# A four-layer graph kernel: the 20-key block in the middle of a part, sums copied head by head, small products as rows, more kept blocks, and two softmax layers in one loop

## The chip, the core and the metric

The kernel runs on one core of one Trainium2 chip. Its time is the device time of one execution in microseconds (us); a kernel's time is the median of several executions. Engines are PE (TensorE), DVE (VectorE), ACT (ScalarE), POOL (GpSimd) and SP (SyncE); the last two are used here mostly to issue DMAs.

## The reference, cut to what matters

`x` is 2708 x 512, `adj` a 0/1 matrix of 2708 x 2708 with ones on its diagonal. Four layers follow each other, each of the form `x = layernorm(x + layer(x, adj))`:

```python
# layer 0, H = 4 heads of width 128; both attention patterns are adj
Xw  = einsum('hnd,hde->hne', Xh, W)
f1  = einsum('hnd,hd->hn', Xw, V[:, 0, :, 0]); f2 = einsum('hnd,hd->hn', Xw, V[:, 1, :, 0])
sig = sigmoid(f1[:, :, None] + f2[:, None, :])
att = masked_softmax(adj * sig)                      # both halves of ALPHA are equal
Xn  = batchnorm(att @ Xw)                            # first pass over att
emb = batchnorm(elu(Xn @ Wenc.T + b) + Xn)
Y   = elu((att @ emb) @ W.T)                         # second pass over att
out = batchnorm(elu(Y @ Wdec.T + b) + Y)
# layer 1
A @ (x @ W + b) / deg[:, None]
# layer 2: h = x @ edge_w, scores h @ h.T, masked by adj, softmax, times node_att and adj
adj * node_att * softmax(where(adj > 0, h @ h.T, NEG_BIG)) @ (x @ weight) + bias
# layer 3
softmax(query @ key.T * scale + adj + adj) @ (x @ Wv + bv)
```

## The kernel before

All matrices are cut into NT = 22 blocks of 128 rows; the last has 20 rows. Layer 0 works in transposed form: a block of 128 keys against half of the queries (HW = 1354 columns, in three chunks of 452, 452 and 450, one PSUM bank each), for two heads at a time. A half and a pair of heads make a *part*; a pass has four of them, in the order (half 0, heads 0-1), (half 0, heads 2-3), (half 1, heads 0-1), (half 1, heads 2-3). In the text `p` is 0 or 1 for the pair of heads.

`project` (L199) computes the values `xw` for the 22 blocks, the rows f1 and f2, and the tile `f1b` in which f1 is spread over all partitions; for the first part this is made by six matmuls (L223). Rows of f1 are also written to `f1_d` in DRAM, from where the later parts load them spread out.

`attention_pass` (L285) runs twice. For each key block it *forms* a tile `t` of 128 x 2 x 1354 (`form`, L309): two Tanh on ACT (L341, the sigmoid written as tanh), one scalar_tensor_tensor on DVE with the block `a` of the adjacency (L349), one Exp on ACT (L350). There are four `t` buffers. In the first pass and for p = 0 the adjacency block comes from the input and is changed first on DVE (L330, L331), then written to `adj_d` on POOL's queue; otherwise it comes from `adj_d`. The blocks listed in `KEPT` are written to DRAM in pass 1 (POOL's queue) and loaded in pass 2 on SP's queue instead of being formed (L390).

Then the products of the block: for each of two heads and three chunks one matmul into `po` (L397), each recorded as two PE instructions[...]. In pass 1 the row sums of `t` come on top (`psm`, L420): for p = 0 of each block; for p = 1 of the first `ALONE` = 6 blocks alone, and after that of two blocks added on DVE (L414). The `po` banks are used by all parts, so a part can begin only when those of the part before have been read.

The reader of `po` is `keep` in pass 1 (L491: six copies, odd chunks on ACT, even ones on DVE, L499) and `decode` in pass 2 (L684: six `take` on DVE, L702). What they leave for later (`scaled`, or `shifted` L715, `turn` L724 and `mlp` L733 with `elu` L431) is done one piece a block in the next part. At the end of the second part of pass 1 `keep` also makes a small matrix-vector product (`small_product` L467: 16 matmuls 128 x 1); two more are made between the passes (`ps_u`, `ps_mean`), where TensorE also transposes and multiplies layer 3's query and key weights (L586, L614) and runs the first dense layer (L637). The last part of pass 2 has no next part: its takes, turns and dense layer run by themselves. Then layer 1's weights are loaded, multiplied with ones (`ps_w1`), centred by four DVE instructions (L847), and the last batch norm is worked out (`batch_scale`, `batch_shift` L461).

Layer 1 starts with L896 (transposes) and L118 (rows times weights), a loop over the adjacency follows (L954).

`softmax_layer` (L1024) is called for layer 2 and again for layer 3, each time with its own pools. It has 7 groups of query blocks and for each 22 key blocks, 154 steps. Scores of a step (L1106; in layer 2 a part of them transposed from scores kept in DRAM, L1098) run 25 steps ahead of the sums of the same group and key (L1213), as the maximum over all keys has to be known. `key_order` puts the 20-row block in the middle. `finish3` writes layer 3's rows on POOL's queue (L1464), from a tile `y` with two buffers.

The order of each engine's work is set by a scheduler that follows the order of the program; an instruction can be tied to another with `tc.issue_after`.

Of the kernel before, what the change touches and what calls it, by code (L numbers as in the profile page):

```python
# [17 lines left out]
P = 128  # L18
# [11 lines left out]
def gnn_stack_kernel(  # L30
# [35 lines left out]
    Q = 32  # L66
# [10 lines left out]
    nc.sync.dma_start(prm_sb, prm)  # L77
# [49 lines left out]
    assert HW <= HB * BANK and NT * P - N < P  # L127
# [14 lines left out]
    ALONE = 6  # L142


    KEPT = [(5, 13, 21), (3, 9, 15, 21)]
# [10 lines left out]
    with ExitStack() as l0:  # L156
# [31 lines left out]
        nc.vector.tensor_scalar(bm1, prm_sb[:, MB_DEC, :], 1.0, None, ALU.subtract)  # L188
        w0T_sb = p0.tile([P, H, P], F32, name="w0T_sb")
        nc.sync.dma_start(w0T_sb, w0T)  # L190
# [8 lines left out]
        def project(att, psum):  # L199
# [5 lines left out]
            nc.sync.dma_start(w0x[:, :, :P], w0)  # L205
            v12 = att.tile([P, H, 2], F32, tag="v12", name="v12", bufs=1)
            nc.sync.dma_start(v12[:, :, 0], v1)
            nc.sync.dma_start(v12[:, :, 1], v2.rearrange("(h e) -> e h", h=H))
            for c in range(C):
                nc.sync.dma_start(xT_sb[:, c, :], xT[c * P : (c + 1) * P, :])  # L210
# [6 lines left out]
            wv1 = held[:, H * (P + 2) : H * (2 * P + 2)].rearrange("p (h e) -> p h e", h=H)  # L217
            nc.vector.tensor_copy(wv1, w0x[:, :, P : P + 1].to_broadcast([P, H, P]))
            f1b = att.tile([P, HP, HW], F32, tag="f1b", name="f1b")
            for k in range(HP):  # L220
                for q, (q0, w) in enumerate(HCH[0]):
                    pf = psum.tile([P, HP, BANK], F32, tag=f"po{q}", name="pf")[:, k, :]
                    nc.tensor.matmul(  # L223
                        pf[:, :w], wv1[:, k, :], xT_sb[:, k, q0 : q0 + w], start=True, stop=True
                    )
                    copy = nc.scalar.copy if q % 2 else nc.vector.tensor_copy
                    copy(f1b[:, k, q0 : q0 + w], pf[:, :w])
            for ci, (c0, w) in enumerate(CHUNKS):
                pf = psum.tile([P, BANK], F32, tag=f"psm{ci % 2}", name="pf")
                for h in range(H):  # L230
                    nc.tensor.matmul(
                        pf[32 * h : 32 * h + 32, :w],
                        wv1[:, h, :32],
# [4 lines left out]
                f1c = att.tile([P, BW], F32, tag="rs", name="f1c")  # L238
                nc.vector.tensor_copy(f1c[:, :w], pf[:, :w])
                nc.gpsimd.dma_start(f1_d[:, c0 : c0 + w], f1c[0 : 32 * H : 32, :w])  # L240
            for jt, (j0, n) in enumerate(BLOCKS):
                pxw = psum.tile([P, H // HP, BANK], F32, tag=f"po{jt % HB}", name="pxw")
                pv = pxw[:, :, : HP * (P + 2)].rearrange("p a (k e) -> p a k e", k=HP)
                for h in range(H):
# [16 lines left out]
                    None,  # L261
                    ALU.mult,
                )
            copies(xw[:, NT - 1, :])
            copies(f2h[:, NT - 1, :])
            return f1b

# [324 lines left out]
        with (  # L592
# [248 lines left out]
            for ci in early:  # L841
                load_x(ci)
# [695 lines left out]
```

## Time and profile before

| | |
|---|---|
| median of 3 executions | 3347.64 us (3344.58 to 3348.74) |
| profiled execution | 3344.3 us, span 3342.5 us, mean granted clock 0.987 |
| first product of pass 1 (L397) | starts at 52.71 us |
| pass 1, to the last 20-row block | 569 us |
| pass 2, to the last part's own work | 692 to 1148.8 us |
| layer 1's first transpose (L896) | 1219.62 us |
| layer 2's softmax | 1684 to 2366.8 us |
| layer 3's first instruction on PE | 2373.57 us |
| last PE work | 3332 us |

The span is the time from the first to the last instruction that the profile records. In the page, the group lines of section 5 give line, engine, operation, tiles, count, then busy time and mean ns of one, and the idle time before them with what ended it. PEclk in section 2 is the clock that TensorE was granted, in tenths of full speed: below 9, the same matmul takes longer. A matmul of 452 columns takes 0.379 us per record at the full clock, counted from start to start.

### The profile page before, as it was taken

What the parts mean: (1) busy time and instruction counts of PE and PEld (TensorE: products, weight loads), DVE (VectorE), ACT (ScalarE), POOL (GpSimd) and SP (SyncE); (2) the same over time, 40 slices, a digit from 0 to 9 for tenths busy, and PEclk for the clock granted to TensorE, in tenths of its full rate; (3) what the DMA queues carried; (4) which work ended last, traced back from release to release, by engine and by line L of the source; (5) the groups of instructions that cost most, each with busy time, mean ns of one, the idle gap of its engine ahead of it and who ended that gap; (6) DMA issues with size and microseconds to landing.
All of it is one profiled execution on the core that took longest, in us unless ns stands there. A gap on an engine that the chain in (4) does not pass through costs nothing.

```text
span 3342.5 us, 30573 instructions
## 1 busy us (share of the span) xinstructions
PE 3251.5 (97%) x10980; PEld 1741.6 (52%) x10980; DVE 1988.9 (60%) x3227; ACT 1347.6 (40%) x1518; POOL 130.7 (4%) x212
## 2 busy tenths in 40 slices
PE   8999999999999989999999999999999999999998
PEld 5444444544444445885555555444455555555554
DVE  7868978767687585445135677776253443443533
ACT  6888887468877652001133333332011010110110
POOL 1100100000000000000010000000000000000001
PEclk9999999999999999999999999999999999999999
DMA  7655753335535412540044444553211111111100
GB/s 284 248 172 187 275 195 102 121 106 185 187 126 166 152 40 76 144 129 15 0 129 127 122 129 131 148 146 95 70 44 36 42 33 42 40 34 45 33 23 20
DMA packets 168576, 367.58 MB, mean 110 GB/s; under 512 B 20870, under 2 KB 111710, under 8 KB 165032
## 3 DMA queue, kind: packets, MB, share of 16 engines
q1 hardware_dynamic: 153448, 301.77, 30.2%
q0 software_dynamic: 14976, 63.86, 5.1%
q8 instruction: 86, 1.41, 0.2%
q14 instruction: 66, 0.54, 0.0%
HBM read 301.67 MB, written 63.35 MB: 109 GB/s over the span
## 4 chain that ended last, share of the span: by engine, by line
PE 72%; issue 13%; DVE 9%; DMA 3%; ACT 3%; POOL 1%; SPq 0%; POOLq 0%; DVEq 0%; ACTq 0%
PE po L1213 21%; PE ps_s L1106 17%; PE po L397 9%; PE ps_nb L954 6%; PE ps_wide L1015 4%; DVE t L349 3%; PE ps_hid L118 2%; PE ps_sup L1356 2%; PE ps_o L1291 2%; PE ps_mlp L637 1%; DMA a<-adj_d 1%; PE ps_dec L733 1%; ACT t L341 1%; DMA a_cols<-in_adjT_dram 1%; ACT t L350 1%
## 5 line engine op out<-in xcount | busy, mean ns | idle before, releaser
L349 DVE SCALAR_TENSOR_TENSOR t<-t,a 128x2708 f32<-128x2708 f32 (+1 forms) x162 | 480.0, 2975 | 142.4 <-ACT t L341 140.4
L341 ACT ACTIVATE t<-f1b,f2h 128x1354 f32<-128x1354 f32 (+1 forms) x324 | 445.8, 1414 | 87.9 <-PE psm L420 42.7
L350 ACT ACTIVATE t<-t 128x2708 f32<-128x2708 f32 (+1 forms) x162 | 396.7, 2452 | 71.1 <-DVE t L349 69.7
L397 PE MATMUL po<-t,xw 128*128 128x452 f32 (+3 forms) x1056 | 416.2, 557 | 8.1 <-ACT t L350 4.0
L397 PE MATMUL po<-t,emb 128*128 128x452 f32 (+3 forms) x1056 | 404.4, 552 | 16.7 <-ACT t L350 9.0
L1213 PE MATMUL po<-sup,e 128*128 128x512 f32 x882 | 410.3, 602 | 5.5 <-DVE e L1400 5.3
L1213 PE MATMUL po<-e,xs 128*128 128x384 f32 (+1 forms) x1176 | 407.5, 489 | 0.0
L1106 PE MATMUL ps_s<-q,hT 128*128 128x384 f32 (+1 forms) x1176 | 403.5, 489 | 0.0
L1454 DVE SCALAR_TENSOR_TENSOR e<-a_cols,ps_s 128x384 f32<-128x384 f32 (+1 forms) x154 | 85.6, 556 | 419.3 <-PE ps_s L1106 396.2
L397 PEld LDWEIGHTS po<-t,emb 128*128 128x128 f32 (+1 forms) x1056 | 195.6, 192 | 218.9 <-issue 195.0
L1106 PEld LDWEIGHTS ps_s<-q,hT 128*128 128x128 f32 x1176 | 222.6, 190 | 161.5 <-issue 6.5
L397 PEld LDWEIGHTS po<-t,xw 128*128 128x128 f32 (+1 forms) x1056 | 190.8, 192 | 220.6 <-issue 201.8
L1213 PEld LDWEIGHTS po<-e,xs 128*128 128x128 f32 x1176 | 221.6, 190 | 157.2 <-issue 6.0
L1213 PEld LDWEIGHTS po<-sup,e 128*128 128x128 f32 x882 | 161.6, 192 | 176.4 <-issue 149.6
L98 ACT ACTIVATE ln_rstd<-ln_rstd 128x1 f32<-128x1 f32 x88 | 17.2, 201 | 494.1 <-DVE ln_rstd L97 493.5
L1106 PE MATMUL ps_s<-hT 128*128 128x384 f32 (+5 forms) x672 | 212.3, 461 | 2.4 <-DVE e L1397 1.7
L1396 ACT ACTIVATE a_cols<-a_cols,neg_big 128x384 f32<-128x384 f32 (+1 forms) x154 | 94.8, 617 | 239.1 <-DMA a_cols<-in_adjT_dram 202.2
L954 PE MATMUL ps_nb<-hid_hi,at 128*128 128x512 f32 x484 | 185.6, 390 | 1.1 <-DVE at L947 1.1
L954 PE MATMUL ps_nb<-hid_lo,at 128*128 128x512 f32 x462 | 179.9, 389 | 0.0
L1190 ACT COPY nmax<-pb 128x384 f32<-128x384 f32 (+1 forms) x14 | 6.7, 480 | 424.9 <-PE pb L1177 345.6
L1208 DVE TENSOR_TENSOR acc<-acc,e 128x384 f32<-128x384 f32 (+2 forms) x294 | 162.5, 553 | 12.2 <-ACT e L1198 2.3
L1106 PEld LDWEIGHTS ps_s<-hT 128*128 128x128 f32 x672 | 122.4, 190 | 88.3 <-issue 17.8
(237 smaller groups left out, 3494.4 us busy)
## 6 DMA issues: line engine op xcount, KB each, us to landing
a<-adj_d SPq DMA_DIRECT2D x116, 677.0 KB
a_cols<-in_adjT_dram SPq DMA_DIRECT2D x378, 192.0 KB
a<-in_adjT_dram SPq DMA_DIRECT2D x42, 677.0 KB
adj_d<-a POOLq DMA_DIRECT2D x42, 677.0 KB, 4.6
raw<-in_adjT_dram SPq DMA_DIRECT2D x105, 256.0 KB
kept<-t POOLq DMA_DIRECT2D x10, 1354.0 KB, 6.5
t<-kept SPq DMA_DIRECT2D x10, 1354.0 KB
a_cols<-in_adjT_dram SPq DMA_DIRECT2D x63, 202.0 KB
```

The source lines that it names most:

```text
L118: nc.tensor.matmul(ps[:n], xt[:, c, :n], w[:, c, :], start=(c == 0), stop=(c == C - 1))
L341: nc.scalar.activation(tv[:, k, :], f1b[:n, k, :w], AF.Tanh, bias=f2h[:n, jt, h : h + 1], scale=0.5,)
L349: nc.vector.scalar_tensor_tensor(tv, tv, GUARD, ab, ALU.add, ALU.mult)
L350: nc.scalar.activation(tv, tv, AF.Exp, scale=0.5)
L397: nc.tensor.matmul(po[HB * k + q][:, :qw], values[r : r + n, jt, h * P : (h + 1) * P], t[r : r + n, k, q0 : q0 + qw], start=(jt == 0), sto ...
L954: nc.tensor.matmul(pos[it], at, half[:, jt, :], start=(jt == 0 and k == 0), stop=(jt == NT - 1),)
L1015: nc.tensor.matmul(ps[:, :width], w(c, o), xt(c), start=(c == 0), stop=(c == C - 1),)
L1106: nc.tensor.matmul(ps[:, b * P : w], keys[:, c, j0 : j0 + P], st["q"][:, c, b * P :], start=(c == 0), stop=(c == C - 1),)
L1208: nc.vector.tensor_tensor(acc, acc, e[:m], ALU.add)
L1213: nc.tensor.matmul(out, lhsT, rhs, start=(k == 0), stop=(k == NT - 1))
L1396: nc.scalar.activation(a, a, AF.Identity, bias=neg_big[: a.shape[0]], scale=1.0e30)
L1454: nc.vector.scalar_tensor_tensor(e, a, 2.0, ps, ALU.mult, ALU.add)
```

## The change

- `project`: the inputs are loaded in another order, `xT` in six column chunks with two adjacency blocks between them. The six spreading matmuls go; f1's rows of the first half are written to `f1_d` and loaded back spread over the partitions. Values of 17 blocks come first; those of the other five, and f1 of the second half, after the first block's DVE step.
- `ORDER`: the 20-row block is taken in place 11 of each part instead of last. `ALONE` is 4, and the last two blocks are also summed alone (`LAST`).
- The form at place 2 is issued after the PSUM copies of the part before (`taken`); the load of `f1b` for the next part after an earlier adjacency load.
- `KEPT`: five places for each pair of heads, one of them the 20-row block: 16 full blocks kept instead of 10.
- `small_product` makes a row of 512 first, copies it, and turns it by four matmuls.
- In the last part `turn` uses the `po` banks, and `centre` (layer 1's weights) runs within it; four groups of layer 1's first instructions are issued after `batch_shift`.
- `softmax_layer` gives back its two step functions. One loop runs both layers; layer 3's scores start 12 steps after layer 2's last score. Layer 3's tiles lie in buffers that layer 2 has left. Its first group takes the keys in their natural order; `y` has four buffers, and the last group's rows leave on SP's queue.

```diff
+    ORDER = list(range(NT // 2)) + [NT - 1] + list(range(NT // 2, NT - 1))
-    ALONE = 6
+    ALONE, LAST = 4, 2
-    KEPT = [(5, 13, 21), (3, 9, 15, 21)]
+    KEPT = [(4, 8, 11, 14, 18), (3, 7, 11, 15, 19)]
+    KEPT = [[ORDER[k] for k in places] for places in KEPT]
...
-            for k in range(HP):
-                for q, (q0, w) in enumerate(HCH[0]):
-                    pf = psum.tile([P, HP, BANK], F32, tag=f"po{q}", name="pf")[:, k, :]
-                    nc.tensor.matmul(
-                        pf[:, :w], wv1[:, k, :], xT_sb[:, k, q0 : q0 + w], start=True, stop=True
-                    )
-                    copy = nc.scalar.copy if q % 2 else nc.vector.tensor_copy
-                    copy(f1b[:, k, q0 : q0 + w], pf[:, :w])
+            for ci, (q0, _) in enumerate(HCH[0]):
+                f1_rows(ci, stage[:, q0:])
+            nc.sync.dma_start(f1_d[:, h0 : h0 + w], stage[0 : 32 * H : 32, :w])
+            spread = nc.sync.dma_start(
+                f1b[:, :, :w], f1_d[:HP, h0 : h0 + w].partition_broadcast(P)
+            )
...
+            AT_ONCE = NT - 5
+            for jt in range(AT_ONCE):
+                values_of(jt)
+
+            def rest(step):
+
+                with tc.issue_after(step.ins):
+                    for jt in range(AT_ONCE, NT):
+                        values_of(jt)
...
-                    for jt, (j0, n) in enumerate(BLOCKS):
+                    for place, jt in enumerate(ORDER):
...
-                            form(hf, p, jt, att, prepare, f1b, t[:rows, :, :w])
+                            with ExitStack() as order:
+
+                                for ins in taken.values() if place == 2 else ():
+                                    order.enter_context(tc.issue_after(ins.ins))
+                                step = form(hf, p, jt, att, prepare, f1b, t[:rows, :, :w])
...
-                        if prepare or jt < ALONE or (jt % 2 == 0 and jt + 1 == NT):
+                        if prepare or not ALONE <= place < NT - LAST:
...
-        def small_product(ps, w, v):
-
+        def small_product(ps, w, v, row):
+
+            for c in range(C):
+                nc.tensor.matmul(
+                    ps[:1, :F], v[:, c : c + 1], w[:, c, :], start=(c == 0), stop=(c == C - 1)
+                )
+            nc.vector.tensor_copy(row, ps[:1, :F])
             for o in range(C):
-                for c in range(C):
-                    nc.tensor.matmul(
-                        ps[:, o : o + 1],
-                        w[:, c, o * P : (o + 1) * P],
-                        v[:, c : c + 1],
-                        start=(c == 0),
-                        stop=(c == C - 1),
-                    )
-            return ps
+                nc.tensor.matmul(
+                    ps[:, o : o + 1],
+                    row[:, o * P : (o + 1) * P],
+                    ones[:1, 0:1],
+                    start=True,
+                    stop=True,
+                )
+            return ps[:, :C]
...
-                        copy(
+                        taken[q % 2] = copy(
                             ft[:, HP * p + k, h0 + q0 : h0 + q0 + qw], po[HB * k + q][:, :qw]
                         )
...
+                    ps = po[HB * k + q]
+                    if not final:
+                        ps = psum.tile([P, BANK], F32, tag="misc", name="ps_y", bufs=2)
...
                     mlp(q, 2, st, True)
+                    if q == 0:
+                        centre(po[0])
                     mlp(q, 3, st, True)
...
+        with tc.issue_after(ready[0].ins):
+            nc.vector.memset(hid_hi[:, NT - 1, :].bitcast(F32), 0.0)
...
-            y = att.tile([P, F], F32, tag="y", name="y3")
+            y = room(17 + it % 4, 1, F)
...
-                nc.gpsimd.dma_start(out[i0 : i0 + n, :], y[:n])
+                queue = nc.sync if it in GROUPS[-1] else nc.gpsimd
+                queue.dma_start(out[i0 : i0 + n, :], y[:n])
...
+        steps = len(GROUPS) * NT
+        lag = NT + AHEAD
+        start3 = steps + 12
+        for t in range(start3 + steps + lag):
+            if t == steps:
+                weights3()
+            if t == steps + lag:
+                values3()
+            if t < steps:
+                score2(t)
+            elif 0 <= t - start3 < steps:
+                score3(t - start3)
+            for first, step in ((lag, sum2), (start3 + lag, sum3)):
+                if 0 <= t - first < steps:
+                    step(t - first)
```

## The prediction

> **What bounds the kernel now.** I read the page's busy times and slices first, then the windows by stage, the groups by line, the waits and time lines around each dark slice, and the chain last.
>
> ```profile
> PE 3251.5 (97%) x10980; PEld 1741.6 (52%) x10980; DVE 1988.9 (60%) x3227; ACT 1347.6 (40%) x1518; POOL 130.7 (4%) x212
> PE   8999999999999989999999999999999999999998
> ...
> 176.00:192.00 16.00, 15.02 (x71) 6.07 (x64) 9.50 (x10) 13.30 (x10) 1.17 (x2) 0.79 0.44 134
> ...
> 305.00:325.00 20.00, 19.74 (x82) 12.29 (x83) 14.46 (x16) 11.67 (x10) 2.24 (x4) 0.66 0.46 153
> ...
> 692.00:1148.80 456.80, 439.35 (x1170) 216.04 (x1172) 329.63 (x269) 372.87 (x246) 1.06 (x2) 0.98 0.48 156
> 1148.80:1220.00 71.20, 60.04 (x156) 28.72 (x151) 61.94 (x108) 23.53 (x40) 0.00 (x0) 0.96 0.31 107
> ...
> 2366.80:2382.00 15.20, 8.68 (x27) 5.51 (x26) 8.23 (x30) 3.36 (x9) 4.67 (x6) 0.66 0.73 229
> ```
>
> TensorE is the bound: 97%, leaving 91 us idle. The window rows (length, then PE, PEld, DVE, ACT, POOL busy, granted clock, DMA share, GB/s) show that this is not all. At the seams of layer 0's parts (176, 305) PE counts as busy, but at a clock of 0.79 and 0.66. The change removes almost no matmul, so its worth lies in idle gaps and half-rate stretches.
>
> ```profile
> PE po L397 <- ACT t L350: 9.0, 6, 2.6
> PE po L397 <- DVE ot L702: 7.8, 3, 3.3
> ...
> 737.65 2.06 PE L397 MATMUL po<-t,emb 128*128 128x452 f32 x5
> 741.84 4.12 PE L397 MATMUL po<-t,emb 128*128 128x452 f32 x6 [2.13 <-ACT t L350]
> ...
> 1039.63 2.25 PE L397 MATMUL po<-t,emb 128*128 128x450 f32 x13
> 1044.86 7.64 PE L397 MATMUL po<-t,emb 128*128 128x452 f32 x13 [2.98 <-DVE ot L702]
> ```
>
> These are waits and PE time lines of pass 2. Two things stop PE: the formed block is late (ACT), or the sums of the part before have not left PSUM (L702). After a stop the next few records take twice their 0.379 us. Counting starts of matmuls against that pitch, a seam costs in all: pass 1 5.3, 8.9 and 5.9 us; pass 2 5.6, 5.9 and 6.3 us; stalls inside pass 2's parts 4.1, 1.0, 1.0, 1.2 and 4.2 us.
>
> ```profile
> L349 DVE SCALAR_TENSOR_TENSOR t<-t,a 128x2708 f32<-128x2708 f32 (+1 forms) x162 | 480.0, 2975 | 142.4 <-ACT t L341 140.4
> L341 ACT ACTIVATE t<-f1b,f2h 128x1354 f32<-128x1354 f32 (+1 forms) x324 | 445.8, 1414 | 87.9 <-PE psm L420 42.7
> L350 ACT ACTIVATE t<-t 128x2708 f32<-128x2708 f32 (+1 forms) x162 | 396.7, 2452 | 71.1 <-DVE t L349 69.7
> ```
>
> Forming a block takes ACT 2 x 1.414 + 2.452 = 5.28 us; pass 2's products take PE 12 x 0.379 = 4.55 us. In a part with 19 formed blocks (p = 0) ACT needs 100.3 us plus about 4 for six Exp of the elu, PE 21 x 4.55 + 1.8 = 97.4 plus about 4.6. ACT is the slower one there.
>
> ```profile
> 1212.81 2.48 DVE xs L847 x4
> ...
> 1215.42 0.48 DVE hid_hi L867
> ...
> 1215.94 1.11 DVE w_sb L876
> ...
> 1219.62 0.45 PE tp_out L896
> ...
> 2373.57 3.45 PE L1005 MATMUL tp<-ident,xs 128*128 128x128 f32 x16 [6.21 <-DVE xs L113]
> ```
>
> Chain and time line: layer 1's weights are centred on the path into layer 1, and layer 3 starts only when layer 2's last normalization is over.
>
> **The change part by part.** Gains against the profiled execution of 3344.3 us (span 3342.5), which lies 3.3 us under the median.
>
> *Start.* Six spreading matmuls (12 records x 0.379 = 4.5 us) go; the rows come back by a broadcast DMA of 1354 KB. PE's first L397 was at 52.71 us, with two blocks' sums (2.75 us) already done: effectively 49.96. Inputs arrive in column chunks, so values start earlier, and only 17 of 22 blocks' values stand ahead of the first product. The new wait is f1b by DMA. From inputs moving at the row's 269 GB/s I estimate f1b at 29.6, the first L349 at 35.5, the first product at 44: gain 6. Bounds: 9 if the broadcast is early; 2 if it comes 4 us late (two adjacency blocks stand ahead of it on SP's queue, the next ones behind). A kept or adjacency write on POOL is not in the way: f1's first half now goes through SP.
>
> *Pass 1 seams.* Before, the last block has 20 rows, 1.79 us of PE instead of 4.55, so the copies L499 get no cover, and ACT's three of them (0.48 each) stand behind Tanh of the next part. After: 20 rows at place 11, the last two blocks summed alone, and the form at place 2 waits for the copies. Banks come free 3.0, 3.8 and 4.55 us into a full last block; two 0.6 us DVE or 0.48 us ACT copies each end at about 5.8 us, under the 1.4 us of row sums that follow. Left: 1 us a seam, and 3 at the second, where the small product sits. As rows it takes PE the same 3.4 us (4 x 512 columns) but at full clock, plus a DVE copy of 0.6 and its semaphores, 1.5 to 2 on a path that nothing covers. Gains 4 + 6 + 5 = 15; the pass's end (1.85 and 1.63 us gaps, part stays) 2; stalls inside p = 1 parts 3. What the added wait delays: ACT's place-2 form, by about 2 us, with all later forms behind it. In p = 1 parts ACT has 117 us of work against PE's 116, so I take 2 us back for each of two such parts: -4. Six more kept writes on POOL hold a t buffer about as long as the existing ones (Tanh waited for such a write 5.5 us in all, ten writes): under 3 us on ACT, covered by PE. Pass 1: 16 (10 to 25).
>
> *Middle.* The two small products as rows, without the half rate after 128x1 matmuls (4.93 us for eight records at 602.8): 2 (0 to 5).
>
> *Pass 2.* Six forms fewer: ACT -31.7 us, DVE -17.9 us. A p = 0 part goes from 19 to 17 forms, 89.8 + 4 on ACT against PE's 102: the bound is PE. The longest run of formed blocks falls from 7 (7 x 0.73 = 5.1 us lost to PE) to 4 (2.9), with up to three blocks in hand. The 20 rows in the middle take PE 1.8 us but are a kept block in every part. Stalls of 11.5 go to about 3: gain 8.5. Seams: before, L702 queued behind L349; with a full block last and 4.55 us of PE ahead the six takes (0.62 each) start earlier. Nothing covers their first pair: PE went on 1.43 us after the takes began (797.73 to 799.16). So 17.8 becomes 3 x 1.4 = 4.2: gain 13.5. Together 22 (12 to 27).
>
> *Rule against row.* The Trainium skill, "TensorE: Matmul & The Clock Gate", Part 1 "The HAM clock gate", says the array drops to half clock after about one 3.4 us window without work, and then runs some 3.4 us at half rate. By it the stops of 2.13 and 2.98 us above would cost only themselves. The rows disagree: six records took 4.12 us behind 2.13 us idle, thirteen 7.64 behind 2.98. On pass 2's stops the slow records alone add 9.5 us. By the rule pass 2 gains 14, by the rows 22; I take the rows. Stops up to 1.13 us left full rate, so the 1.4 us I leave at each seam should stay cheap.
>
> *Last part.* w1's product (3.43 us) and its four L847 (2.48) move among the elu work of the last part. PE has 11 us idle there and takes the product for nothing; DVE is busy 61.94 of 71.2 us, so of 2.48 I charge 1.5 (up to 5 if PE's product also lies on the path). L847, the memset 0.48, the copy 1.11 and two L947 (0.75) leave the path: 4.8, of which I count 3.1 since the copy is still needed. The takes start 1.5 us earlier and the 2.33 us stop with its half rate (4.1) shrinks by 2.5: 3.1 + 2.5 - 1.5, net 4 (0 to 8). turn() in po banks instead of misc frees two PSUM banks; I count nothing for it, as the takes release po just ahead.
>
> *Layers 2 and 3 in one loop.* Layer 3's scores start before layer 2's sums end, so the 10.8 us lost at 2366.8 go (6.37 gap, the rest half rate): 9 (7 to 10.5). The reordered weight loads come hundreds of us after their buffers are free. L3's first spread of maxima (6.6 lost) stays.
>
> *Tail.* Four y buffers remove a POOL wait of 1.8 us that was mostly hidden, the last stores leave by SP: 1.5 (0.5 to 2.5).
>
> Layer 1 and the other groups: order unchanged, 0.
>
> Sum: 6 + 16 + 2 + 22 + 4 + 9 + 1.5 = 60.5. 3344.3 - 60.5 = 3283.8; plus 3.3 to the median: 3287.
>
> **The rivals.** *Seams stay.* Takes and copies again stand behind an L349, stops stay over 2 us, half rate with them. For it: DVE is 72% busy in pass 2, in order. Against it: the explicit wait at place 2. Pass 1 and 2 then give 10 instead of 38: gain about 32, 3315.
>
> *The change doesn't do what it says.* The waits end at another instruction than those named, so only the start, the merge and the tail count: 16.5, 3331.
>
> *Slower: kept reloads become exposed.* Sixteen reloads of 1354 KB on SP's in-order queue each wait for a t buffer, with the next adjacency loads behind them. A buffer frees three blocks (13.65 us) before its use; these DMAs land in 5.4 us (median; at most 9.8). Exposure starts at 13.65, and the kernel turns slower when the mean exposure passes 60.5 / 16 = 3.8 us, a landing of 17.4 us. At 20 us: 16 x 6.35 = 102 lost, 3389. Against it: pass 2 moves 156 GB/s at a DMA share of 0.48 and would rise to about 165.
>
> **How the numbers follow.** Differences under about 0.2% (6.7 us) can't be told from none. Main case 0.63, 3266 to 3300; seams stay 0.22, 3300 to 3325; only start, merge, tail 0.09, about 3331; a near cancellation 0.03; exposed reloads 0.03. Faster 0.94, same 0.03, slower 0.03. The range takes the main case's edge from below (3262: unknown costs at their good ends) and most of the seams case: 3262 to 3320.
>
> **What would show it.** Right: granted clock near 1.00 where the parts meet; no L702 or L499 wait over 1.5 us; layer 1's first product (1219.62 before) at about 1170, earlier by the 50 us of layer 0's parts; no gap before layer 3's first product; ACT under 350 us busy in pass 2. Wrong: first L397 after 50 us; PE waiting for a t loaded from DRAM; ACT as releaser inside p = 1 parts of pass 1 for more than 4 us; the last part longer than 71 us.

## The result: 27 us faster, less than half of what was forecast

| | before | changed | ratio, 95% interval |
|---|---|---|---|
| median | 3346.11 us (4 executions) | 3318.66 us (4) | 0.9921 [0.9905, 0.9937] |
| profiled execution's span | 3342.5 us | 3317.5 us | |

The changed kernel ran once more among the last experiments: 3320.15 us, 0.9917 [0.99, 0.9933]. The forecast was 3287. The number of the rival "seams stay" (3315) is near, but of its six seams only two went its way, and the largest loss was another.

Lines of the page of the changed kernel, then of its windows, its waits in pass 1 and in the stretch after that, and its PE time line:

```profile
PE 3232.7 (97%) x10920; PEld 1725.2 (52%) x10920; DVE 1971.7 (59%) x3221; ACT 1319.5 (40%) x1497; POOL 130.1 (4%) x211
```

```profile
172.90:190.00 17.10, 17.10 (x80) 7.57 (x80) 11.87 (x7) 16.38 (x11) 1.74 (x3) 1.00 0.58 180
299.00:319.00 20.00, 10.99 (x36) 4.39 (x27) 15.99 (x17) 9.48 (x6) 2.56 (x5) 0.74 0.52 168
692.90:1140.20 447.30, 434.92 (x1173) 213.89 (x1173) 313.37 (x265) 343.78 (x228) 1.05 (x2) 0.99 0.51 172
1140.20:1204.80 64.60, 57.12 (x150) 27.84 (x148) 59.05 (x104) 23.84 (x41) 0.00 (x0) 0.96 0.29 99
2398.00:2414.00 16.00, 16.00 (x66) 9.04 (x66) 12.48 (x40) 4.43 (x10) 2.44 (x3) 1.00 0.15 38
```

```profile
PE po L460 <- ACT t L394: 15.7, 6, 8.2
PE psm L483 <- DVE t L477: 3.7, 3, 1.4
```

```profile
PE po L460 <- ACT t L394: 9.1, 7, 5.8
PE tp_out L985 <- DVE ot L979: 7.5, 1, 7.5
PE po L460 <- DVE ot L814: 3.2, 1, 3.2
```

For comparison, two waits of the kernel before in its start and pass 1 (50 to 600 us):

```profile
PE po L397 <- ACT t L350: 4.0, 7, 1.0
PE po L397 <- ACT ft L499: 4.0, 2, 3.1
```

The windows show both sides. Pass 1's first seam (172.9) has full clock and no idle time, and so has the place where layer 2 meets layer 3 (2398): those two are repaired. The second seam (299) is worse than before, with PE busy 11 of 20 us. In the waits of pass 1, products that wait for a formed block (L460 for L394) have taken the place of products that wait for the sums to leave PSUM. The waits of pass 2 look the same, but their longest one (5.8 us) is put down to the wrong engine, as shown below.

By stages, from starts of matmuls (in the start and pass 1, 2.75 us of row sums that lay ahead of the first product before are counted as pass 1; parts are in the order of the text):

| stage | before | changed | difference | forecast |
|---|---|---|---|---|
| to the first product of pass 1 | 50.0 | 43.3 | -6.7 | -6 |
| pass 1 | 521.9 | 528.6 | +6.7 | -16 |
| middle | 120.1 | 121.0 | +0.9 | -2 |
| pass 2, four parts | 107.2, 109.9, 135.8, 104.0 | 108.0, 107.9, 128.3, 103.1 | -9.5 | -22 |
| last part, to layer 1's first transpose | 70.8 | 64.7 | -6.1 | -4 |
| layer 1 | 304.1 | 304.7 | +0.6 | 0 |
| from layer 1's end to layer 3's first sums | 950.7 | 944.6 | -6.1 | -9 |
| layer 3 to its last projection | 857.2 | 857.2 | 0 | 0 |
| after that | 10.9 | 6.2 | -4.7 | -1.5 |

But for rounding, the differences add up to the 25.0 us between the two spans. Two rows carry the error: pass 1 (22.7 us) and pass 2 (12.5 us).

### The profile page after: what moved, and what is told of

The parts are those of the page before. It is cut to its first block, busy times and chain, and to the rows that moved or that the text cites. A ratio compares the mean times of both kernels' runs of the same rounds, so it can differ in the third digit from the quotient of the medians.

```text
span 3317.5 us, 30401 instructions
## 1 busy us (share of the span) xinstructions
PE 3232.7 (97%) x10920; PEld 1725.2 (52%) x10920; DVE 1971.7 (59%) x3221; ACT 1319.5 (40%) x1497; POOL 130.1 (4%) x211
## 4 chain that ended last, share of the span: by engine, by line
PE 76%; DVE 9%; issue 8%; DMA 4%; ACT 3%; POOL 0%; SPq 0%; DVEq 0%; POOLq 0%; ACTq 0%
PE po L1310 22%; PE ps_s L1203 17%; PE po L460 11%; PE ps_nb L1044 6%; PE ps_wide L1105 4%; DVE t L393 3%; PE ps_hid L117 2%; PE ps_sup L1447 2%; PE ps_o L1388 2%; PE ps_mlp L713 2%; PE ps_dec L848 2%; DMA a<-adj_d 1%; ACT t L394 1%; DMA a_cols<-in_adjT_dram 1%; PE psm L483 1%
## 5 line engine op out<-in xcount | busy, mean ns | idle before, releaser
L393 DVE SCALAR_TENSOR_TENSOR t<-t,a 128x2708 f32<-128x2708 f32 (+1 forms) x156 | 462.1, 2974 | 125.0 <-ACT t L385 121.1
L385 ACT ACTIVATE t<-f1b,f2h 128x1354 f32<-128x1354 f32 (+1 forms) x312 | 428.1, 1413 | 61.7 <-PE po L460 28.0
L460 PE MATMUL po<-t,xw 128*128 128x452 f32 (+3 forms) x1056 | 415.1, 557 | 15.7 <-ACT t L394 15.7
L394 ACT ACTIVATE t<-t 128x2708 f32<-128x2708 f32 (+1 forms) x156 | 382.5, 2454 | 110.5 <-DVE t L393 110.3
L460 PE MATMUL po<-t,emb 128*128 128x452 f32 (+3 forms) x1056 | 400.3, 547 | 12.4 <-ACT t L394 9.1
L1203 PE MATMUL ps_s<-sup,hT 128*128 128x384 f32 (+1 forms) x1176 | 406.9, 490 | 0.0
L460 PEld LDWEIGHTS po<-t,xw 128*128 128x128 f32 (+1 forms) x1056 | 191.2, 192 | 228.4 <-issue 201.7
L1203 PEld LDWEIGHTS ps_s<-sup,hT 128*128 128x128 f32 x1176 | 221.9, 190 | 164.2 <-issue 14.1
L460 PEld LDWEIGHTS po<-t,emb 128*128 128x128 f32 (+1 forms) x1056 | 193.5, 190 | 212.1 <-issue 187.3
L1294 DVE TENSOR_TENSOR e<-e,nmax 128x384 f32<-128x384 f32 (+1 forms) x308 | 154.5, 551 | 21.8 <-ACT nmax L1287 21.8
```

Of the source, the lines that this page charges most:

```text
L385: nc.scalar.activation(tv[:, k, :], f1b[:n, k, :w], AF.Tanh, bias=f2h[:n, jt, h : h + 1], scale=0.5,)
L393: step = nc.vector.scalar_tensor_tensor(tv, tv, GUARD, ab, ALU.add, ALU.mult)
L394: nc.scalar.activation(tv, tv, AF.Exp, scale=0.5)
L460: nc.tensor.matmul(po[HB * k + q][:, :qw], values[r : r + n, jt, h * P : (h + 1) * P], t[r : r + n, k, q0 : q0 + qw], start=(place == 0), ...
L1203: nc.tensor.matmul(ps[:, b * P : w], keys[:, c, j0 : j0 + P], st["q"][:, c, b * P :], start=(c == 0), stop=(c == C - 1),)
L1294: nc.vector.tensor_tensor(e, e, st["nmax"][:, :w], ALU.add)
```

## The experiments

Every edit is against the changed kernel unless it is said otherwise. The table gives the stages that differ, in us, from the profile of each; "(1)" is a single execution. Profiles of kernels with the same pass 1 show how far its second part varies by itself (137.2 to 139.9).

| kernel | pass 1, four parts | middle | pass 2, four parts | median | ratio to before |
|---|---|---|---|---|---|
| changed | 129.6, 139.9, 132.3, 126.8 | 121.0 | 108.0, 107.9, 128.3, 103.1 | 3318.66 | 0.9921 [0.9905, 0.9937] |
| e1 row out of z | 129.6, 127.0, 132.7, 126.2 | 120.6 | 108.1, 107.9, 128.4, 102.9 | 3312.18 | 0.9889 [0.9874, 0.9904] |
| e2 20 rows last in pass 1, p = 1 | 129.6, 131.5, 132.2, 118.8 | 124.0 | 108.2, 108.1, 128.3, 103.2 | 3307.57 | 0.9878 [0.9862, 0.9895] |
| e4 places 10 and 11 alone | 129.6, 136.2, 131.7, 123.9 | 120.3 | 108.2, 109.4, 128.3, 103.0 | 3313.89 | 0.9895 [0.9880, 0.9910] |
| e5 = e1 and e2 | 129.9, 118.6, 139.0, 117.7 | 124.4 | 108.4, 107.9, 128.4, 103.1 | 3302.67 | 0.9864 [0.9848, 0.9881] |
| e8 no added wait | 129.6, 142.9, 133.5, 125.9 | 121.1 | 108.2, 109.5, 129.4, 103.0 | 3321.58 | 0.9919 [0.9904, 0.9934] |
| e3 other kept places | 130.9, 139.8, 132.7, 126.5 | 120.7 | 106.0, 106.6, 128.8, 103.1 | 3323.94 | 0.9929 [0.9915, 0.9944] |
| e6 20 rows last in pass 2 | 129.6, 139.1, 132.2, 124.3 | 121.2 | 105.5, 109.6, 134.3, 105.4 | 3326.14 | 0.9934 [0.9919, 0.9949] |
| e7 10 kept | 129.6, 137.2, 132.7, 126.3 | 120.8 | 110.5, 107.2, 138.1, 108.1 | 3335.22 | 0.9962 [0.9949, 0.9975] |
| e9 last rows by POOL | 129.7, 137.2, 132.8, 126.5 | 120.9 | 108.2, 109.2, 128.0, 103.0 | 3323.33 (1) | |
| e10 middle's products in columns | 129.7, 137.3, 132.7, 126.3 | 121.7 | 108.0, 109.4, 129.7, 102.8 | 3318.20 (1) | |
| e11 no counting | 129.8, 137.3, 132.8, 126.6 | 118.2 | 106.0, 109.2, 128.7, 102.7 | 3315.37 (1) | |
| e12 = e5, takes first | 129.6, 118.6, 138.6, 117.9 | 123.7 | 103.9, 106.9, 131.0, 108.2 | 3302.30 | 0.9870 [0.9852, 0.9887] |
| e13 = e5, last of p = 0 kept | 129.6, 118.6, 139.9, 117.7 | 122.9 | 105.7, 110.5, 128.5, 103.9 | 3300.34 | 0.9858 [0.9843, 0.9873] |
| e14 = e13, six kept for p = 1 | 129.6, 124.2, 134.4, 117.9 | 122.8 | 105.5, 113.1, 129.5, 102.1 | 3299.66 | 0.9858 [0.9840, 0.9876] |
| e16 = e13, no counting | 129.6, 118.5, 138.8, 117.7 | 121.1 | 102.9, 107.2, 128.4, 102.6 | 3291.13 (1) | |
| e17 = e13, counting in pass 1 | 137.3, 121.9, 146.9, 122.7 | 120.6 | 102.9, 107.2, 128.1, 102.6 | 3314.98 | 0.9893 [0.9875, 0.9910] |

### Pass 1: a shared buffer, and a short block in the middle

The second seam of the changed kernel, first DVE, then PE (start, length, instructions, and in brackets the idle time before and what ended it):

```profile
284.44 2.97 DVE L393 SCALAR_TENSOR_TENSOR t<-t,a 128x2708 f32<-128x2708 f32 x1
296.56 1.16 DVE L569 COPY ft<-po 128x452 f32<-128x452 f32 x2 [9.15 <-PE po L460]
...
302.78 0.68 DVE L538 COPY row<-po 1x512 f32<-1x512 f32 x1 [2.70 <-PE po L535]
304.59 0.16 DVE L575 TENSOR_TENSOR enc_bias<-po,prm_sb 128x4 f32<-128x4 f32 x1 [1.14 <-PE po L540]
304.68 0.87 DVE L374 TENSOR_SCALAR z<-a 128x1354 f32<-128x1354 f32 x1
305.58 1.57 DVE L375 SCALAR_TENSOR_TENSOR a<-z,a 128x1354 f32<-128x1354 f32 x1
```

```profile
303.51 1.05 PE L540 MATMUL po<-ones,row 1*128 1x1 f32 x8 [0.77 <-DVE row L538]
312.80 6.31 PE L460 MATMUL po<-t,xw 128*128 128x452 f32 x12 [8.24 <-ACT t L394]
```

DVE stands idle for 9.15 us and prepares the next half's first block (L374, L375) only when the small product is over. Before, that preparation (L330 there) ran while the last blocks of the part were multiplied, ahead of the copies:

```profile
301.47 0.86 DVE L330 TENSOR_SCALAR z<-a 128x1354 f32<-128x1354 f32 x1
...
305.14 1.14 DVE L499 COPY ft<-po 128x452 f32<-128x452 f32 x2
```

The row of the new small product is a tile with the tag of `z`, of which there is one buffer: the next writer of `z` has to wait until the row is read. From 304.68 the chain of the first block is 0.87 + 1.57 us, a short reciprocal, 2.91 (L393) and 2.46 us (Exp), and PE stands still for 8.24.

```diff
-                    row = att.tile([P, HW], F32, tag="z", name="row", bufs=1)[:1, :F]
+                    row = ft[:1, C - 1, N - F :]
```

> The changed kernel, but the row of the small product at the end of the first p = 1 part lies in a free corner of ft instead of the single z buffer. Theory A (z is the cause: DVE cannot prepare the next half's first blocks until the row is read, so PE waits 8.4 us for the first formed block): that wait falls to under 2 us and the kernel is 8 to 11 us faster than the changed kernel, about 3308 us. Theory B (ACT or the added wait at place 2 is the cause): the wait stays over 6 us and the time within 2 us of 3318.

The second part fell to 127.0 us, against 137.2 to 139.9 with the shared buffer: 10 to 13 us. Theory A stands. The stop itself is gone: no gap over 0.4 us is left at that seam. The median fell less, to 3312.18; the parts are those of the profiled execution, which at 3307.26 us was the fastest of the four.

The other loss in pass 1 shows in both p = 1 parts. Before, their inside lost 8.4 and 5.8 us against full rate (starts of matmuls, 192 to 302.7 and 464 to 567); in the changed kernel 13.0 and 13.6 (190 to 298, 462 to 570.4), with the same gaps in both parts:

```profile
228.91 6.53 PE L460 MATMUL po<-t,xw 128*128 128x452 f32 x24
236.85 2.08 PE L483 MATMUL psm<-t,ones 128*32 128x340 f32 x16 [1.41 <-DVE t L477]
238.87 10.28 PE L460 MATMUL po<-t,xw 128*128 128x452 f32 x24
...
270.97 1.35 PE L483 MATMUL psm<-t,ones 128*32 128x340 f32 x16
275.01 5.29 PE L460 MATMUL po<-t,xw 128*128 128x452 f32 x9 [2.69 <-ACT t L394]
```

The 24 records that take 6.53 us are a full block and the 20-row block. PE is through with 20 rows in 1.8 us, so the addition of the pair (2.97 us on DVE) is not covered; and ACT needs 5.28 us for those 20 rows as for any block, so its lead shrinks, and some 37 us later PE waits for a block. (In between ACT itself waits twice for a `t` buffer, 2.55 and 1.55 us.)

```diff
-                    for place, jt in enumerate(ORDER):
+                    for place, jt in enumerate(range(NT) if first and p else ORDER):
```

> The changed kernel, with the 20-row block last again in the two p = 1 parts of pass 1 only (all else as changed, the last two places summed alone). Theory C (the 20-row block in the middle costs 5 us a part there: its pair addition is not covered and ACT loses its lead): the stretch inside each p = 1 part loses 6 to 8 us instead of 13, and the two seams after them lose 3 to 5 us more, so the time changes by less than 6 us either way. Theory D (the middle place is harmless, the losses come from six more kept writes): the inside still loses 12 us or more and the seam gets worse, 3325 or more.

```diff
-                        if prepare or not ALONE <= place < NT - LAST:
+                        if prepare or not ALONE <= place < NT - LAST or place in (10, 11):
```

> The changed kernel with places 10 and 11 of the p = 1 parts of pass 1 summed alone instead of as a pair: one addition less (2.9 us on DVE), one group of row sums more (1.35 us on PE) per part. If the addition is what stops PE at the 20-row block (1.85 us and half rate behind it, 4.3 us in all), each such part gets 2 to 3 us shorter, 4 to 6 in all. If ACT's lead is what is lost, the wait only turns from the addition to the Exp and the parts stay within 1 us.

With the 20 rows last (e2) the two parts took 131.5 and 118.8 us, 6 to 8 us less each, and the middle 3.0 more. Neither expectation had the size: the inside came down as theory C says, but the seams after the parts gave little of it back, and the kernel was 11 us faster. Theory D falls; e7 below, with fewer kept writes, has the same p = 1 parts as the changed kernel (137.2 and 126.3) and speaks against it too. With the pair split (e4) they took 136.2 and 123.9: 0.4 to 4 us less each, although that kernel has one more group of row sums (1.3 us) in each. The time lost inside the two parts fell by 5.0 and 4.5 us with the pair split, and by 8.6 and 7.8 with the 20 rows last. So the uncovered addition is half of this loss or more. ACT's lead is what is left, by difference; no run takes it away alone.

> The changed kernel with both repairs: the small product's row out of the z buffer, and the 20-row block last in the p = 1 parts of pass 1. If the two losses are separate (12.9 us in the second part; 8 us in each p = 1 part, of which the middle gives 3 back), the parts of pass 1 take 129.6, about 119, 132.5 and 119 us, and the kernel about 3295 us. If the z wait only hid the one behind the other, the second part stays above 124 and the kernel above 3301.

e5 has both repairs, as diffs above: 118.6 and 117.7 us, and the third part 139.0, since a part of the small product now lies behind its first product. All of pass 1 took 505.2 us, 16.7 less than before the change.

```diff
-                                for ins in taken.values() if place == 2 else ():
+                                for ins in ():
```

> The changed kernel without the added wait: the form at place 2 is not tied to the PSUM copies, so these stand one block further back on ACT and DVE. If the wait makes the seams of pass 1, each of its first and third seams (5.3 and 5.9 us before, 1.2 after) loses 3 to 5 us again, 6 to 10 us in all; what it takes back by delaying ACT inside the p = 1 parts (my -2 us a part) comes off that. If the place of the 20-row block alone covers the copies, the time stays within 3 us of 3318.

Without the added wait (e8) the second part took 142.9 us, 3 more than the longest of the others; the third and fourth moved by about 1 in both directions. The two medians are not told apart. No gap over 0.6 us came back at the first and third seams, which speaks for the second theory there: the full block in the last place covers the copies.

### Pass 2: two things hold the same seam

In the changed kernel the third seam is clean; PE stops at the first two. The profile puts the first stop down to ACT, the second to the takes:

```profile
790.29 4.82 PE L460 MATMUL po<-t,emb 128*128 128x452 f32 x12 [1.15 <-ACT t L394]
800.87 6.31 PE L460 MATMUL po<-t,emb 128*128 128x452 f32 x12 [5.77 <-ACT t L394]
```

```profile
903.51 2.06 PE L460 MATMUL po<-t,emb 128*128 128x452 f32 x5
908.78 7.24 PE L460 MATMUL po<-t,emb 128*128 128x452 f32 x14 [3.21 <-DVE ot L814]
```

But the first stop is for the takes as well. DVE and ACT there:

```profile
793.88 1.57 DVE L335 TENSOR_SCALAR_CACHE_REDUCE z<-a 128x1354 uint8<-128x1354 f32 x1 [4.03 <-DMA a<-adj_d]
...
795.37 2.98 DVE L393 SCALAR_TENSOR_TENSOR t<-t,a 128x2708 f32<-128x2708 f32 x1
798.26 3.66 DVE L814 SCALAR_TENSOR_TENSOR ot<-po,bn_scale,rb 128x452 f32<-128x452 f32 x6
```

```profile
787.80 4.79 ACT L394 ACTIVATE t<-t 128x2708 f32<-128x2708 f32 x2
...
798.38 2.46 ACT L394 ACTIVATE t<-t 128x2708 f32<-128x2708 f32 x1 [1.84 <-DVE t L393]
```

Counted off by formed blocks, the second Exp at 787.80 is that of the next part's first block (place 0). It was ready at 792.59, 8.3 us before PE took it up. The Exp at 798.38 is that of place 1. It starts with the takes, behind the same multiplication, and ends (800.84) 0.1 us after the fourth of them (800.73), so the two can be mistaken for each other. Other kernels below tell them apart: at this seam PE takes up place 0 in e3 again 0.15 us after the fourth take, but 0.9 us before the Exp of place 1 ends (802.45 against 803.31), and in e12 after the second take and 9 us before. Why the fourth take counts in some kernels and the second in others is open. What makes the takes late is the multiplication of place 1 in front of them on DVE (795.37). In front of that stands the count of zeros (L335) in a later adjacency block (by the order of the loads that of place 4), which was loaded only at 793.76.

```diff
-                    for place, jt in enumerate(ORDER):
+                    for place, jt in enumerate(ORDER if first else range(NT)):
```

> The changed kernel with the 20-row block last in all parts of pass 2 (it is one of the kept blocks either way). By my forecast its place in the middle is worth the cover of the takes, about 4.5 us at each of three seams: pass 2 goes from 447.3 to about 460. If it is worth nothing, as in the p = 1 parts of pass 1, pass 2 stays at 447 or gets shorter.

```diff
-    KEPT = [(4, 8, 11, 14, 18), (3, 7, 11, 15, 19)]
+    KEPT = [(5, 11, 13), (3, 9, 11, 15)]
```

> The changed kernel with as many kept blocks as before the change: places (5, 11, 13) and (3, 9, 11, 15), 10 full blocks instead of 16. By my forecast six more kept blocks are worth about 8 us of stalls in pass 2: pass 2 grows from 447.3 to 455 or more, mostly in its p = 0 parts; pass 1 gets up to 3 us shorter since fewer writes hold a t buffer. If kept blocks are not what decides, pass 2 stays within 3 us.

```diff
-    KEPT = [(4, 8, 11, 14, 18), (3, 7, 11, 15, 19)]
+    KEPT = [(3, 8, 11, 16, 20), (2, 6, 11, 15, 19)]
```

> The changed kernel with other kept places: (3, 8, 11, 16, 20) and (2, 6, 11, 15, 19) instead of (4, 8, 11, 14, 18) and (3, 7, 11, 15, 19), as many blocks kept. Runs of formed blocks that cross a seam fall from 6 (last three of p = 0, first three of p = 1) to 4, and from 6 to 5 at the seam after p = 1. Theory E (ACT falls behind over the run that crosses the seam): the stop of 5.9 us at pass 2's first seam falls under 2 us and pass 2 gets 6 to 12 us shorter than 447.3. Theory F (the takes and adjacency loads are the cause): pass 2 stays within 3 us of 447.3.

The 20 rows in the middle are worth 7.5 us in pass 2 (e6: 454.7), where I had about 13. Kept blocks are worth more than forecast: with ten of them (e7) pass 2 took 464.0 us, 16.7 more, and more than the 456.8 of the kernel before. In e7 the last kept place is 13 or 15, so that up to eleven formed blocks follow each other over a seam; the number and the places are not separated in it. Before, the kept 20-row block was the last of a part and gave ACT a rest exactly there. Other places (e3) made pass 2 2.8 us shorter; the first seam's stop fell from 5.9 to 3.2 us, still for the takes (L814), with 3.3 us of new waits ahead of it. Theory F's number holds, E's does not, although the run over that seam is only three blocks long there (the expectation says four).

```diff
-                if not first and p == (jt in KEPT[0]):
-                    count(hf, jt, att, a)
...
-                            if p == 0 and jt in KEPT[1]:
-                                count(hf, jt, att)
```

> The changed kernel without the counting of zeros in pass 2 (44 DVE instructions of 1.57 us; the degrees that layer 1 divides by are then wrong, nothing else is left out). If DVE is what makes the formed blocks late in pass 2, the 5.9 and 3.4 us stops at its first two seams go and pass 2 falls from 447.3 to about 436. If ACT alone is the cause (run of six formed blocks over the seam), the first seam's stop stays over 4 us and pass 2 over 443.

This kernel leaves out the degrees that layer 1 divides by. Pass 2 took 446.7 us and the first stop lost 5.8 us. By its expectation ACT alone is the cause, and so says the chain of waits in this kernel: from 763.94 to 795.51 it runs through Tanh, the multiplication and Exp without a DMA, and the time line of ACT is full. The multiplication of place 1 now waits for its Tanh, and the takes behind it:

```profile
784.92 1.41 ACT L383 ACTIVATE t<-f1b,f2h 128x1354 f32<-128x1354 f32 x1
786.24 2.44 ACT L392 ACTIVATE t<-t 128x2708 f32<-128x2708 f32 x1
788.59 4.04 ACT L383 ACTIVATE t<-f1b,f2h 128x1354 f32<-128x1354 f32 x3
793.04 2.46 ACT L392 ACTIVATE t<-t 128x2708 f32<-128x2708 f32 x1 [0.42 <-DVE t L391]
```

Two kernels on top of e5 then tried what stands at the seam. In e12 `got` holds the last of the takes (L814), and in pass 2 the form at place 1 is issued after it; e13 keeps one more block inside ACT's run:

```diff
-                                for ins in taken.values() if place == 2 else ():
+                                for ins in taken.values() if place == (2 if first else 1) else ():
...
-            attention_pass(emb, False, att, psum, decode)
+            attention_pass(emb, False, att, psum, decode, taken=got)
...
-    KEPT = [(4, 8, 11, 14, 18), (3, 7, 11, 15, 19)]
+    KEPT = [(4, 8, 11, 14, 18, 21), (3, 7, 11, 15, 19)]
```

> The kernel with both repairs, and in pass 2 the form at place 1 of a part issued after the six takes of the part before, as pass 1 does at place 2. If the takes behind two adjacency multiplications make the second seam's stop (3.2 us), it falls under 2 us and pass 2 gains 3 to 5 us, about 3298 us in all. If the forms that now come later are what PE needs next, PE waits for ACT instead and pass 2 gets longer than 447 us.

> The kernel with both repairs, and the last place of the p = 0 parts (21) kept as well: 18 full blocks. The run of formed blocks over the seams after p = 0 falls from 6 to 3 and leaves one more block in ACT's hand. If that run is what stops PE, the 6 us stop at pass 2's first seam falls under 2 us, and pass 2 shortens from 447.8 to about 440 (that seam and the third); pass 1 changes by less than 2 us; about 3294 us in all. If not, pass 2 stays within 3 us.

Pass 2's waits in e12:

```profile
PE po L460 <- ACT t L394: 8.9, 10, 1.9
PE ps_y L841 <- DVE ot L829: 3.7, 3, 2.4
PE po L460 <- DVE ot L816: 1.7, 1, 1.7
```

Here PE took up place 0 of the second part at 775.50, right after the second take, 9 us before the Exp of place 1 ended (784.79): PE had stood for the takes. The first two stops fell from 6.0 and 3.1 us (e5) to 1.7 and 0.4. But now the multiplication of place 1 came behind the takes, and PE waited for that block (1.9 us) and at `ps_y` for `shifted` (3.7 us in all). Against e5 the first two parts of pass 2 became 5.5 us shorter, the last two 7.7 longer: the stops moved, and the sum did not fall.

e13 did not confirm ACT's run: the stop lost 4.8 us instead of 6. But its chain is another one:

```profile
764.38 2.99 DVE t L393
767.37 0.02 issue
767.39 3.93 DMA a<-adj_d
...
771.43 0.13 DVE z L335
...
773.00 2.90 DVE t L393
775.90 0.02 issue
775.92 2.47 ACT t L394
```

A multiplication (L393) frees one of three `a` buffers, the next adjacency block is loaded into it (3.93 us), its zeros are counted on DVE (L335, 1.57 us), and the multiplication of the next part's second block, with the takes behind it, stands behind that count. The chain of the changed kernel itself has the same pieces at this seam (a load of 3.89 us at 789.87, the count, the multiplication). So there are two chains of nearly the same length that hold back one multiplication, and taking away either leaves the other.

> e13 (last place of the p = 0 parts kept, both repairs) without the counting in pass 2, which leaves only the degrees of layer 1 out. If ACT's run of six and DVE's counting behind an adjacency load hold the first seam side by side, its stop (5.8 us with ACT's run alone, 4.8 with the counting alone) falls under 2 us here, and pass 2 is 8 us or more shorter than e13's 448.6. If a third thing holds it (the takes, the adjacency load itself), the stop stays over 3 us and pass 2 over 444.

Both taken away: the stop lost 3.1 us, pass 2 took 441.0 us, 7.6 less than e13 and 6.8 less than e5 has with both (one execution; e17 below has the same 440.8). On its own the kept block had changed pass 2 by 0.8 us the wrong way, and the missing count had taken off 0.6. That the two hold the seam side by side is shown; that 3 us stay (by the chain Tanh and the multiplication of place 1, the takes again behind it) was not forecast. The second seam grew to 5.1 us, for the takes. Both orders of takes and multiplication cost something at a seam (e5, e12); a better one is open.

e14 is e13 with `(3, 7, 11, 15, 17, 20)` for p = 1:

> As e13, with (3, 7, 11, 15, 17, 20) kept for p = 1: 20 full blocks, and the run over the seam after p = 1 is 21 and 0 to 3, five instead of six, with a kept block close before it. If runs over a seam decide, the second seam's stop (3.2 us and half rate) shrinks too, pass 2 about 436; but here takes on DVE stand ahead of PE as well, so it may stay near 3. The kernel then lies between 3288 and 3296 us.

Pass 2 took 450.3 us: the second seam's stop grew to 6.2 us. The kernel stood at 3299.66; e13, e14, e12 and e5 can't be told apart by their intervals.

e17 has e13's kept blocks and does the counting by L374's sum over the row:

```diff
-                    nc.vector.tensor_scalar(z[:n, :w], a[:n, :w], 0.0, None, ALU.is_equal)
+                    nc.vector.tensor_scalar(
+                        z[:n, :w], a[:n, :w], 0.0, None, ALU.is_equal, ALU.add,
+                        accum_out=zeros[:n, jt, hf : hf + 1],
+                    )
```

> e13 with the zeros counted in pass 1, by the DVE instruction that compares with zero there (0.86 us; with a sum over its row I estimate 1.57, as the count of pass 2 has). Pass 2 as in e16. The p = 0 parts of pass 1 get 22 x 0.7 = 15 us more DVE work on some 116 of 130 us busy; if DVE then sets their length, each grows by 2 to 6 us. With 8 us gained in pass 2 the kernel would stand at 3292 to 3300 us.

Pass 2 took 440.8 us, as in e16, but the p = 0 parts of pass 1 took 137.3 and 146.9: 7 or 8 us each, above the forecast 2 to 6, and the p = 1 parts 3 to 5 more. The kernel is slower than e13.

The changed kernel ran beside these:

> The changed kernel as it is, beside the others: 3318 us, the parts of pass 1 at 129.6, 137 to 140, 132.5 and 126.5 us and pass 2 at 447 to 449.

It gave 3320.15 us, with 129.6, 138.9, 131.7, 124.7 in pass 1 and 447.9 in pass 2. On the same chip e13 stood at 0.9858 [0.9843, 0.9873] and e14 at 0.9858 [0.9840, 0.9876] of before, the changed kernel at 0.9917 [0.9900, 0.9933]: with the two repairs of pass 1 the kernel is about 20 us faster than the changed one.

### Middle and tail

```diff
-                queue = nc.sync if it in GROUPS[-1] else nc.gpsimd
+                queue = nc.gpsimd
```

> The changed kernel with the last group's rows leaving by POOL's queue again (four y buffers stay). The time after the last product of layer 3 was 10.9 us before and 6.1 in the changed kernel; I had forecast 1.5 us for the buffers and the queue together. If the queue is the cause, this stretch is 9 to 11 us here; if the buffers are, it stays under 7.5.

The stretch after the last projection took 10.7 us, against 6.2 with the other queue (and 6.1 to 6.6 in all other kernels here). The queue is the cause; the four buffers are worth 0.1. Time lines of e9 (POOL) and of the changed kernel (DVE):

```profile
3314.58 0.52 POOL L1592 DMA_DIRECT2D out_dram<-sup  x1 [2.91 <-DVE sup L112]
```

```profile
3314.35 0.53 DVE L112 TENSOR_SCALAR sup<-sup,ln_mv,ln_rstd 20x512 f32<-20x512 f32 x1
```

The changed kernel ends at 3317.5, 2.7 us after that DVE instruction. In e9 the last store is issued just as early, but the kernel ends at 3321.5: SP is through at 3316.7, POOL, which issued the store, only at 3320.8.

e10 has the two small products of the middle as 16 one-column matmuls again:

> The changed kernel with the two small products between the passes in the old form (16 matmuls of one column each), the one in pass 1 as rows. My forecast was that rows save 2 us in the middle: it would take 123 us instead of 121. If the trip over DVE (row copied before it is turned; two waits of 1.6 and 0.9 us in the changed kernel) eats what full rate gives, the middle stays within 1 us of 121.

The middle took 121.7 us, against 120.3 to 121.2 in the other kernels that keep the changed order in pass 1 and the count: the second theory. In the changed kernel the row's trip over DVE makes PE wait 1.4 us at `ps_u`, about what the half rate had cost.

## Why the prediction failed, step by step

- *Start, last part, layers 2 and 3:* right in kind, and within 3 us in size (-6.7, -6.1, -6.1 against -6, -4, -9). Layer 2's end and layer 3's start now share full clock, and of the 10.8 us lost there 8.1 show in the time; 2 us are given back where layer 2's projections start (PE waits 2.6 us for L1098, before 0.6). The cause of that wait is open.
- *Pass 1 seams:* the step that failed is the second seam, "3 at the second, where the small product sits". I priced the row's copy and its semaphores, and not the buffer in which the row lies. The diff shows it (`tag="z"`, one buffer), and the writer that was queued behind it is L374: DVE stood idle for 9.15 us. It cost 10 to 13 us (e1). The first and third seams came out as forecast: 5.3 and 5.9 us before, 1.2 each after.
- *Pass 1, p = 1 parts:* "stalls inside p = 1 parts 3" and "I take 2 us back for each" had the wrong size. The 20-row block costs ACT 5.28 us and gives PE 1.8 us; I weighed that for pass 2, where it is loaded and not formed, and not for pass 1, where it is formed and where the addition of its pair has only those 1.8 us of cover. It cost 6 to 8 us a part (e2), where I had 0.5 us on balance. With both repaired, pass 1 gained 16.7 us where I had 16. That agreement is luck: the 20 rows then stand where they stood before in the p = 1 parts, and the middle gave 3 to 4 us back.
- *Pass 2:* the step that failed is the term of the seams, "the six takes (0.62 each) start earlier ... So 17.8 becomes 3 x 1.4". Counted alike in both kernels (from the start of each record to the next, against its usual pitch), the three seams lost 16.0 us before and 13.3 in the changed kernel, the stretches between them 13.1 and 6.2. So the stalls gave 7 of the 8.5 us, the seams under 3 of the 13.5. At two of the three seams the takes still stood behind a multiplication, and at the first seam that one was late for two reasons. The first reason is in "the longest run of formed blocks falls from 7 to 4": I counted runs inside a part. Over the seam after p = 0 they are six long (places 19 to 21, 0 to 2), and before the change the kept last block stood there. The second reason, the count of zeros in a later block ahead of it on DVE, has no term in my sum. As single changes the two measures don't add up: with ten kept blocks alone (e7) pass 2 took 464.0 us, with the 20 rows last (e6) 454.7, before 456.8, with both measures 447.3; and of e7's 16.7 us, its long run and its number of kept blocks are not separated.
- *Rule against row:* in the changed kernel the rows held: a stop of 3.21 us is followed by 14 records in 7.24 us, and one of 1.15 by twelve in 4.82, which is full rate. But the length of a stop doesn't settle it alone: in e16 a stop of 2.94 us is followed by twelve records in 4.79 us, full rate too.
- *Tail:* 1.5 was mis-sized; the queue alone measured 4.6 us (e9). *Middle:* 2 measured 0, since I counted the row's way over DVE in pass 1 and left it out here.
- *The added wait:* I charged -4 us for it. e8, without it, was not faster.
- *Rivals:* "seams stay" came true at two seams of six, both in pass 2, and its time was near the measured one mostly because of what pass 1 lost elsewhere. My argument against it, "the explicit wait at place 2", holds for pass 1 only: pass 2 is called without `taken`. The exposed reloads did not come: no wait of PE ended with a kept block loaded from DRAM. The landing of "5.4 us (median; at most 9.8)" that I took for them is that of the kept writes on POOL's queue; the profile shows no landing of the reloads.
- *Signs:* ACT came to 343.8 us in pass 2, under the 350 that I had named, while two seams stayed: the sum of an engine's work doesn't show whose wait ends last. Of the signs of being wrong one came: ACT stopped PE inside the p = 1 parts of pass 1 for 6.4 us.

## What to carry to other kernels

When a new tile takes an existing tag, list who writes that tag next, and what that engine does meanwhile: one buffer shared for a moment at a seam held DVE for 9 us and PE for 8. Check a wait that the profile names against the time at which the thing waited for was ready: here the block had been ready for 8 us. Count runs of costly blocks over the seam of two parts, not inside one; and a short block can cost its elementwise engines a full block (here 5.28 us of ACT for 20 rows), so it should stand where they are ahead, or be loaded. If taking away one cause changes nothing, read the chain again in that very kernel: a second one of equal length may have stood beside it, and only both together show.

## What was not expected of the hardware

How late POOL ends after its last DMA: 5.7 us from the end of that issue (3315.1) to POOL's last wait at the program's end (3320.8), where the store itself landed in 1.8 us (the median that the DMA view gives for e9's 40 KB store). The kernel before shows the same: the issue ended at 3336.6, the store landed at 3337.9, POOL's last wait ended at 3341.7. By SP's queue the kernel ended 2.7 us after the last computation.
